# A graph convolution on one core: the two finishing stages of a chunk in their own memory bank, and the copy of a chunk's sum ahead of the next scalings

## The chip, the cores and the metric

The kernel runs on one core of a Trainium2 chip. The metric is the device time of one execution in microseconds (us); lower is better. The engines are TensorE (PE: matmuls; its weight loads are PEld), VectorE (DVE), ScalarE (ACT), GpSimd (POOL) and SyncE (SP). Each runs its own list of instructions in order, and instructions of different engines wait for each other through semaphores. Here SP issues ordinary DMA transfers and POOL issues the gathers (indirect DMAs, one for 128 rows). Matmuls write to PSUM, which ACT and DVE read.

## What is computed

A residual network on a graph of 6250 nodes with 128 features and 200000 edges sorted by their target node. Two layers follow each other: a graph attention layer, and an equivariant convolution. The change touches the second alone. Cut to what matters, with `x0`, `x1` linear maps of the normalized node features:

```python
e0 = f0[edge_src]; e1 = f1[edge_src]             # gather of source rows, 32 scalars and 32 vectors
h = gelu(gelu(edge_scalar_attr @ W_mlp1 * c) @ W_mlp2 * c2)
w = einsum('pxu,ex->epu', W_tp, h) * c2          # four weights per channel and edge
m0 = w[:, 0] * e0 * a0[:, None]                  # a0: first edge attribute, a1: the other three
m1 = w[:, 3] * einsum('eui,ei->eu', e1, a1) * INV_SQRT3
m2 = w[:, 1, :, None] * e0[:, :, None] * a1[:, None, :]
m3 = w[:, 2, :, None] * e1 * a0[:, None, None]
agg = zeros((N, 256)).at[edge_dst].add(concatenate([m0, m1, m2, m3], axis=1))
out = x + [COS * self + SIN * agg @ Wf]          # per irreducible part
```

## The kernel before, in words

The attention layer takes the first 2310 us or so and is the same in both kernels. Then a short stage builds a table of 128 values per node, and the edge loop of the convolution follows (L1632 to L1657), from about 2430 us to the end.

**Tiles.** A tile is 128 edges; there are NT = 1563. A group is SB = 8 tiles (196 groups), and one pass of the loop works on one group. A chunk is CT = 24 tiles, three groups; the 66 chunks cover 66 ranges of target nodes. I call the three groups of a chunk the first, second and third.

**One group.** `fetch` (L1611) gathers the source rows into a buffer `G` (L353, eight gathers on POOL; six buffers) and lets ACT scale them by `a0` (`scaled`, L1492, eight activations at L1495, result `g`). `layers` (L1588) loads the edge scalars `a8t` (L1595, two DMAs on SP, four buffers) and starts `hidden` (L1467), whose two layers are a matmul (L1476) into a PSUM bank with the tag "layer" (two buffers) and a Gelu on ACT (L1479, `hid`) each. `weigh` (L1483) turns the second layer's result into the weights, 8 pairs of matmuls (L1488) into a bank `big` (two buffers). `messages` (L1498) is DVE's part: seven instructions from L1508 to L1517; L1512 is the first that reads `big`, into a small tile `w`. The result `mess` has three buffers. `one_hot3` (L1523) compares target numbers with a row of slots. `scatter` (L1528) adds the messages with 8 pairs of matmuls (L1531) into the chunk's sum `whole` in PSUM, of which there is one.

**One chunk.** The first group of the next chunk closes a chunk: `close` (L1558) copies the sum to `acc` on ACT (L1561), and loads the chunk's own node features `xb` (L1564). The seventh tile of the next chunk adds the part of that sum that belongs to its nodes (`sink`, L1569; L1577 on DVE, L1579 on PE). `finish3` (L1533) is a generator in two stages. The first transposes the sum by matmuls (L1539) and copies it on ACT (L1541, `at`). The second multiplies by the last weights (L1544), adds `xb` by a matmul with the identity (L1545), copies on ACT (L1547, `o`, one buffer) and issues the output DMA (L1548). Both stages get their PSUM from outside: the bank `pw` that the weigh of the same pass then writes too, at other columns of the same tile.

**Order.** Most instructions are recorded through `keep`, which makes each engine run them in the order of the program. In one pass that order is: messages, the second layer of an earlier group, the first layer of group g+4, `fetch` of group g+1, a waiting stage of `finish3`, `close` where a chunk ends, `weigh` for group g+2, scatter. So ACT runs in the first group of a chunk: eight scalings, the copy of the sum, two activations; in the second: scalings, `at`, two activations; in the third: scalings, `o`, two activations. A stage's matmuls stand ahead of weigh on PE. SP runs its list in order too: two loads of `a8t` per group, and the loads of `xb`, the loads of attributes `a4` (L1603) and the output DMAs between them.

Of the kernel before, what the change touches and what calls it, by code (L numbers as in the profile page):

```python
# [31 lines left out]
F32 = mybir.dt.float32  # L32
# [11 lines left out]
P = 128  # L44
# [6 lines left out]
CT, LT = 24, 40  # L51
# [13 lines left out]
def gnn_kernel(ctx: ExitStack, tc: tile.TileContext, x, src, dst, attr4, attr8,  # L65
# [4 lines left out]
    N, D = x.shape  # L70
# [29 lines left out]
    NCH = -(-NT // CT)  # L100
# [14 lines left out]
    def big():  # L115
        return ps_big.tile([P, 8, P], F32, tag="big", name="big")
# [1080 lines left out]
    for now in range(NGR * MS + 1):  # L1197
        g, m = divmod(now, MS)
# [112 lines left out]
    with tc.tile_pool(name="att2", bufs=1) as pool, tc.tile_pool(name="dense", bufs=2) as dense, \  # L1311
# [68 lines left out]
        for b0 in range(0, NB, 2):  # L1380
            n = min(2, NB - b0)
# [13 lines left out]
            for h0 in range(0, NB, HS):  # L1395
# [7 lines left out]
                c = ct[:, :n, :, h0:h0 + HS, :].rearrange("p k a h d -> p h (k a) d")  # L1403
                parts = [t[:, :, :n * P].rearrange("p h (a d) -> p h a d", d=QN) for t in (ramp, up, down)]
# [14 lines left out]
            parts = dense.tile([P, 2, 2, R2], F32, name="parts")  # L1419
            acc = acc[:, :n, :2 * C2].rearrange("p k (j c) -> p k j c", j=2)  # L1420
            for k in range(n):
                b = b0 + k
# [28 lines left out]
    cw = ctx.enter_context(tc.tile_pool(name="cw", bufs=2))  # L1451
# [4 lines left out]
    ps_kept = ctx.enter_context(tc.tile_pool(name="ps_kept", bufs=1, space=PSUM))  # L1456
# [26 lines left out]
    def weigh(n, hid, pw):  # L1483

        for j in range(min(n, NPR)):
            for c in range(j, n, NPR):
                half = slice(c // NPR * HID, (c // NPR + 1) * HID)
                keep(nc.tensor.matmul(pw[:, c, :], hid[half, j * P:(j + 1) * P],  # L1488
                           wtp_sb[half].rearrange("x p u -> x (p u)"), start=True, stop=True))
        return pw  # L1490
# [39 lines left out]
            acc, start, stop = sink(c)  # L1530
            keep(nc.tensor.matmul(acc, oh[:, c, :], ms[:, c].rearrange("e h i u -> e (h i u)"), start=start, stop=stop))  # L1531

    def finish3(parts, xb, to):  # L1533


        ps = yield
        for j in range(2):
            for i, a in enumerate(parts):
                keep(nc.tensor.matmul(ps[:, j, :], a[:, j * D:(j + 1) * D], ident, start=i == 0, stop=i == len(parts) - 1))  # L1539
        at = cw.tile([P, 2, D], F32, name="at")  # L1540
        keep(nc.scalar.copy(at, ps[:, :2, :]))  # L1541
        ps = yield
        for j in range(2):
            keep(nc.tensor.matmul(ps[:, 0, :], at[:, j, :], wo_sb[:, j, :], start=j == 0, stop=False))  # L1544
        keep(nc.tensor.matmul(ps[:, 0, :], ident, xb, start=False, stop=True))  # L1545
        o = cw.tile([P, D], F32, name="o", bufs=1)
        keep(nc.scalar.copy(o, ps[:, 0, :]))  # L1547
        nc.sync.dma_start(to, o[:to.shape[0], :])  # L1548
        yield

    with tc.tile_pool(name="conv", bufs=1) as pool, tc.tile_pool(name="gath3", bufs=6) as gath:
        def first_node(c):
            return nc.values_load(base_i[0:1, c:c + 1], engines=[SP], min_val=0, max_val=N - P,
                                  skip_runtime_bounds_check_because="clamped to this range where it is computed")

        state, todo = {}, deque()

        def close(c):  # L1558

            a = cw.tile([P, 2 * D], F32, name="acc3")  # L1560
            keep(nc.scalar.copy(a, state["acc"]))  # L1561
            state["sums"] = [a]
            xb = cw.tile([P, D], F32, name="xb")
            nc.sync.dma_start(xb, xtd[ds(first_node(c), P), :])  # L1564
            ending = finish3(state["sums"], xb, out[ds(first_node(c), P), :])
            next(ending)
            todo.extend([ending, ending])

        def sink(t):  # L1569
            c, k = divmod(t, CT)  # L1570
# [11 lines left out]
        groups = [(t, min(SB, NT - t)) for t in range(0, NT, SB)]  # L1582

        def hots(g):
            t, n = groups[g]
            return one_hot3(dstc[:, t:t + n], n, cw.tile([P, SB, P], F32, name="ohr", bufs=4))

        def layers(g):  # L1588
            if g >= len(groups):
                return iter(())  # L1590
            t, n = groups[g]
            a8t = cw.tile([2 * NRAD, NPR * P], F32, name="a8t", bufs=4)
            for j in range(2 if n > NPR else 1):
                c = (t + j * NPR) * P
                nc.sync.dma_start(a8t[j * NRAD:(j + 1) * NRAD, :], attr8_t[:, c:c + NPR * P])  # L1595
            return hidden(n, a8t)
# [8 lines left out]
        def keep_a1(t):  # L1605
            m = min(LT, NT - t)
            a1s = kept[:, P + t // LT % 2 * 3 * LT:P + (t // LT % 2 + 1) * 3 * LT].rearrange("p (k f) -> p k f", f=3)
            keep(nc.vector.tensor_copy(a1s[:, :m], a4s[t][:, :m, 1:]))
            return a1s

        def fetch(g):  # L1611
            t, n = groups[g]
            if t % LT == 0 and t + LT < NT:
                load_a4(t + LT)
            G = gath.tile([P, SB, D], F32, tag="G", name="G")
            gather(G, table3, srcc[:, t:t + n], n)
            return G, scaled(G, n, a4s[t // LT * LT][:, t % LT:t % LT + n, 0:1])
# [3 lines left out]
        hids, pws = deque(), deque()  # L1621
# [10 lines left out]
        for g, (t, n) in enumerate(groups):  # L1632
            G, g0 = rows
            i = t % LT
            last = g + 1 == len(groups)
            ms, after = messages(G, g0, n, a1s[:, i:i + n, :], pws.popleft(), None if last else lambda: hots(g + 1),
                                 lambda: None)
            if i + SB == LT and t + SB < NT:
                a1s = keep_a1(t + SB)
            next(second, None)  # L1640
            first = layers(g + 4)
            next(first, None)
            if not last:
                rows = fetch(g + 1)
            weighing = hids.popleft() if hids else None
            pw = big() if weighing is not None or todo else None
            if todo:
                todo.popleft().send(pw)
            if t and t % CT == 0:
                close(t // CT - 1)  # L1650
            hids.extend(list(second)[-1:])
            next(first, None)
            if weighing is not None:
                pws.append(weigh(groups[g + 2][1], weighing, pw))
            scatter(ms, oh, range(n), lambda c: sink(t + c))
            second = first
            oh = after  # L1657
        close(NCH - 1)
        while todo:
            todo.popleft().send(big())  # L1660

        tot3 = pool.tile([P, 2 * D], F32, name="tot3")
        base = pool.tile([P, 1], F32, name="base")

        def general3(b, n):
            nc.vector.tensor_copy(base, starts[:, ds(b, 1)])
            nc.vector.memset(tot3, 0.0)
            with tc.For_i(0, NCHUNK, 1) as i:
                si, di = load_chunk(i)
                dl = work.tile([P, GK], F32, name="dl")  # L1670
                nc.vector.tensor_scalar(dl, di, base, None, op0=OP.subtract)
                at = []
                for f, attr in ((4, attr4), (NRAD, attr8)):
                    t = cw.tile([P, GK, f], F32, name=f"a{f}g")
                    nc.vector.memset(t, 0.0)
                    nc.sync.dma_start(t[:GP], attr[ds(i * (GP * GK), GP * GK), :].rearrange(
                        "(p k) f -> p k f", p=GP))
                    at.append(t)
                acc = whole()[:, :2 * D]
                for s in range(0, GK, GSB):  # L1680
                    cs = slice(s, s + GSB)
                    G = gath.tile([P, SB, D], F32, tag="G", name="Gg")
                    gather(G, table3, si[:, cs], GSB)
                    pa = big().rearrange("p c u -> p (c u)")
                    for c in range(GSB):
                        nc.tensor.transpose(pa[:NRAD, c * P:(c + 1) * P], at[1][:, s + c, :], ident)
                    a8t = cw.tile([2 * NRAD, NPR * P], F32, name="a8t", bufs=4)
                    nc.scalar.copy(a8t[:NRAD, :GSB * P], pa[:NRAD, :GSB * P])
                    pw = weigh(GSB, list(hidden(GSB, a8t))[-1], big())
                    ms, oh = messages(G, scaled(G, GSB, at[0][:, cs, 0:1]), GSB, at[0][:, cs, 1:], pw, lambda: one_hot(  # L1690
                        dl[:, cs], GSB, cw.tile([P, SB, P], F32, name="ohr", bufs=4)), lambda: None)
                    scatter(ms, oh, range(GSB), lambda c: (acc, s + c == 0, s + c == GK - 1))
                nc.vector.tensor_add(tot3, tot3, acc)
            xb = cw.tile([P, D], F32, name="xb")
            nc.vector.tensor_copy(xb, xt[:, ds(b, 1), :].rearrange("p o f -> p (o f)"))
            ending = finish3([tot3], xb, out[ds(b * P, n), :])
            next(ending)
            for _ in range(2):
                ending.send(big())

        with tc.If(flag_of(again3[0:1, 0:1]) > 0):
            with tc.For_i(0, FULL, 1) as b:
# [72 lines left out]
```

## Time and profile before

| what | value |
|---|---|
| median of 3 runs | 4809.09 us (4805.12 to 4830.14) |
| profiled execution, its own time | 4877.21 us |
| its span, first to last instruction | 4875.4 us |
| mean granted TensorE clock | 0.799 |
| attention and preparation | to about 2430 us |
| edge loop, full chunks | 2432.8 to 4802.5 us |
| its end | 4802.5 to 4875.4 us |
| PE, DVE, ACT, POOL busy, share of the span | 66%, 60%, 50%, 51% |
| gathers of the convolution (L353) | 1563, of 946 ns each |

The profile is one execution. It is about 1.4% longer than the median; durations are taken from it, and sums are made against its own time first. The profile's groups give for each line its instructions, busy time, the mean of one, and the idle time of the engine before them with what ended it. A releaser is inferred from semaphores; "remote" stands where the trace has no event for it, and "issue" where the engine waited for nothing that is seen. The timeline lists instructions with start and duration in us, and in brackets the idle time ahead and its releaser. Ends of matmuls are modelled.

### The profile page before, as it was taken

What the parts mean: (1) busy time and instruction counts of PE and PEld (TensorE: products, weight loads), DVE (VectorE), ACT (ScalarE), POOL (GpSimd) and SP (SyncE); (2) the same over time, 40 slices, a digit from 0 to 9 for tenths busy, and PEclk for the clock granted to TensorE, in tenths of its full rate; (3) what the DMA queues carried; (4) which work ended last, traced back from release to release, by engine and by line L of the source; (5) the groups of instructions that cost most, each with busy time, mean ns of one, the idle gap of its engine ahead of it and who ended that gap; (6) DMA issues with size and microseconds to landing.
All of it is one profiled execution on the core that took longest, in us unless ns stands there. A gap on an engine that the chain in (4) does not pass through costs nothing.

```text
span 4875.4 us, 63641 instructions
## 1 busy us (share of the span) xinstructions
PE 3212.9 (66%) x21302; PEld 2421.0 (50%) x21303; DVE 2937.8 (60%) x4901; ACT 2425.5 (50%) x5811; POOL 2501.5 (51%) x2440
## 2 busy tenths in 40 slices
PE   3247667777667789997466566665666666665667
PEld 3135545555445578886244444444444444444445
DVE  5457888888778779997244444444444444444445
ACT  3228788878778769997222222222322222222233
POOL 3556666657555600001655655555655555555553
PEclk7558888888788879998677777777787777877778
DMA  3346666767566554442111111111111111111111
GB/s 100 89 123 170 176 178 178 186 174 194 158 161 173 160 216 160 173 173 94 44 48 49 48 48 48 48 47 49 49 50 48 47 48 47 49 48 49 47 48 30
DMA packets 420347, 491.22 MB, mean 101 GB/s; under 512 B 267937, under 2 KB 303628, under 8 KB 419998
## 3 DMA queue, kind: packets, MB, share of 16 engines
q1 hardware_dynamic: 340900, 345.68, 23.8%
q0 software_dynamic: 78304, 139.36, 12.2%
q8 instruction: 175, 2.87, 0.2%
q10 hardware_dynamic: 794, 1.88, 0.1%
q14 instruction: 174, 1.43, 0.1%
HBM read 383.20 MB, written 103.42 MB: 100 GB/s over the span
## 4 chain that ended last, share of the span: by engine, by line
PE 23%; another core or an unknown queue 22%; ACT 4%; issue 3%; DVE 0%; DMA 0%; ACTq 0%; DVEq 0%
PE whole L1531 12%; PE layer L1476 5%; PE big L1488 4%; ACT g L1495 3%; ACT hid L1479 1%; PE big L1539 1%; PE whole L1579 1%; ACT o L1547 0%; PE big L1544 0%; ACT at L1541 0%; PE big L1545 0%; DVE mess L1517 0%; DMA out_x<-o 0%; ACT L1479 0%
## 5 line engine op out<-in xcount | busy, mean ns | idle before, releaser
L353 POOL DMA_INDIRECT G<-table,srcc x1563 | 1478.4, 946 | 1581.1 <-issue 626.5
L353 POOL DMA_INDIRECT G<-table,srcw x808 | 962.7, 1192 | 619.4 <-DVE msg L394 293.6
L1531 PE MATMUL whole<-mess,ohr 128*128 128x256 f32 x3126 | 838.6, 423 | 36.4 <-issue 24.6
L1488 PE MATMUL big<-wtp_sb,hid 64*128 64x128 f32 x3126 | 292.4, 335 | 856.3 <-ACT o L1547 739.6
L1512 DVE TENSOR_TENSOR w<-big,G 128x256 f32<-128x256 f32 x196 | 82.5, 421 | 1283.8 <-PE big L1488 764.9
L1096 ACT ACTIVATE up<-erb,sel 128x512 bf16<-128x512 f32 x1176 | 813.3, 744 | 1.0 <-PE small L878 1.0
L1531 PEld LDWEIGHTS whole<-mess,ohr 128*128 128x128 f32 x3126 | 648.6, 213 | 167.1 <-issue 41.7
L1488 PEld LDWEIGHTS big<-wtp_sb,hid 64*128 64x128 f32 x3126 | 245.3, 232 | 937.3 <-ACT o L1547 750.7
L878 PE MATMUL small<-key,lo 128*128 128x98 bf16 x3136 | 314.4, 231 | 379.2 <-issue 163.2
L860 ACT CAST ca<-small 128x392 bf16<-128x392 f32 x784 | 387.9, 498 | 297.6 <-remote 134.6
L1547 ACT COPY o<-big 128x128 f32<-128x128 f32 x66 | 17.6, 266 | 1038.4 <-remote 976.5
L878 PEld LDWEIGHTS <-lo 128*128 128x128 bf16 x3136 | 285.2, 123 | 469.9 <-issue 436.3
L1011 PE MATMUL up<-up,rc 128*102 128x512 bf16 x1176 | 474.5, 436 | 42.5 <-DVE up L1020 12.2
L1495 ACT ACTIVATE g<-G,a 128x128 f32<-128x128 f32 x1563 | 478.0, 401 | 0.0
L1401 ACT ACTIVATE ramp<-erb,sel 128x256 bf16<-128x256 f32 (+1 forms) x1138 | 461.1, 517 | 14.3 <-DVE up L1409 8.0
L1020 DVE TENSOR_TENSOR up<-up,ctc 128x3584 bf16<-128x3584 bf16 x168 | 339.5, 2021 | 59.6 <-issue 26.0
L1160 PEld LDWEIGHTS whole<-msg,ohr 128*128 128x128 f32 x1616 | 332.3, 244 | 62.8 <-issue 21.7
L852 DVE TENSOR_TENSOR lo<-slots,turned 128x2048 bf16<-128x2048 bf16 x196 | 238.8, 1218 | 162.9 <-PE small L878 72.3
L1160 PE MATMUL whole<-msg,ohr 128*128 128x68 f32 x1616 | 326.5, 317 | 1.3 <-ACT ring L1166 0.8
L1479 ACT ACTIVATE hid<-layer 128x512 f32<-128x512 f32 x392 | 220.7, 601 | 159.1 <-remote 63.8
L1014 PE MATMUL every<-ctc,rc 128*103 128x512 bf16 x588 | 256.4, 436 | 1.1 <-issue 1.0
L1414 PE MATMUL big<-rhs,up 128*128 128x196 bf16 x2401 | 239.8, 250 | 9.6 <-DVE up L1409 9.0
(316 smaller groups left out, 5112.8 us busy)
## 6 DMA issues: line engine op xcount, KB each, us to landing
counts<-ca SPq DMA_DIRECT2D x196, 392.0 KB
ct<-counts SPq DMA_DIRECT2D x196, 392.0 KB
ctc<-counts SPq DMA_DIRECT2D x1344, 56.0 KB
rc<-rhs SPq DMA_DIRECT2D x84, 358.8 KB
oht<-dlow SPq DMA_DIRECT2D x50, 512.0 KB
G<-table,srcc POOLq DMA_INDIRECT x1563
G<-table,srcw POOLq DMA_INDIRECT x808
a8t<-attr_rows SPq DMA_DIRECT2D x391, 16.0 KB
```

What stands on the lines that cost most here:

```text
L353: nc.gpsimd.indirect_dma_start(out=G[:, c, :], out_offset=None, in_=table, in_offset=bass.IndirectOffsetOnAxis(ap=idx[:, c:c + 1], axis=0))
L860: nc.scalar.copy(ca[:, :, k * W:(k + WBANK) * W].rearrange("p h (k d) -> p h k d", d=W), ps[:, :WBANK * NKEY].rearrange("p (k h d) -> p h ...
L878: nc.tensor.matmul(ps[:, n * NKEY:(n + 1) * NKEY], lo[:, a, :, r], ky[:, a, :, r], start=True, stop=True)
L1011: nc.tensor.matmul(sums["ups"][j][:2 * C1, :], r[:, i, c:c + 2 * C1], up[:, i], start=h0 + i == 0, stop=h0 + i == NB - 1)
L1020: nc.vector.tensor_tensor(by_part, by_part, state["ct", p, h0].rearrange("p k a h d -> p h (k a) d"), op=OP.min)
L1096: nc.scalar.activation(up[:, i], state["erb", p][:, j], AF.Relu, bias=sel1[:, h0 + i, 2 * q + j:2 * q + j + 1], scale=STEEP)
L1160: nc.tensor.matmul(kept1["acc"], ohs[g][:, t, :], mss[g][:, t], start=g * SB + t == first_of(c), stop=g * SB + t + 1 == last_of(c))
L1401: nc.scalar.activation(ramp[:, h, :n * P], erb[:, :n * P], AF.Relu, bias=sel2[:, h0 + h, :], scale=STEEP)
L1479: keep(nc.scalar.activation(x[:, :npr * P], ph, AF.Gelu_apprx_tanh, scale=1.0 / math.sqrt(size)))
L1488: keep(nc.tensor.matmul(pw[:, c, :], hid[half, j * P:(j + 1) * P], wtp_sb[half].rearrange("x p u -> x (p u)"), start=True, stop=True))
L1495: keep(nc.scalar.activation(g0[:, c], G[:, c, :], AF.Copy, scale=a0[:, c, :]))
L1531: keep(nc.tensor.matmul(acc, oh[:, c, :], ms[:, c].rearrange("e h i u -> e (h i u)"), start=start, stop=stop))
```

## The change

`finish3` takes its PSUM from the layers' two banks (`small_bank`), in place of the bank of weigh. Its stages are taken up at fixed passes: one, two and six passes after the pass that closes the chunk (`todo` is a dictionary by pass, `proceed`), and each stands after weigh and before the scatter of its pass. At the sixth only the output DMA is issued; `o` has two buffers. `close`, with the copy of the sum on ACT and the load of `xb`, now stands ahead of `fetch` of the next group, so ACT's order is, in the first group of a chunk: the copy of the sum, eight scalings, two activations; in the second: scalings, two activations, `at`; in the third: scalings, two activations, `o`. The counts of matmuls, activations and DMAs stay. The address of the output is formed when its DMA is issued (`place`). What the general path `general3` calls is adapted; it isn't run with these inputs.

```diff
-    def finish3(parts, xb, to):
-        ps = yield
+    def small_bank():
+        bank = ps_kept.tile([P, 4 * P], F32, tag="layer", name="layer", bufs=2)
+        return bank.rearrange("p (j f) -> p j f", f=P)
+
+    def finish3(parts, xb, place):
+        yield
+        ps = small_bank()
         for j in range(2):
             for i, a in enumerate(parts):
                 keep(nc.tensor.matmul(ps[:, j, :], a[:, j * D:(j + 1) * D], ident, start=i == 0, stop=i == len(parts) - 1))
         at = cw.tile([P, 2, D], F32, name="at")
         keep(nc.scalar.copy(at, ps[:, :2, :]))
-        ps = yield
+        yield
+        ps = small_bank()
...
-        o = cw.tile([P, D], F32, name="o", bufs=1)
+        o = cw.tile([P, D], F32, name="o", bufs=2)
         keep(nc.scalar.copy(o, ps[:, 0, :]))
+        yield
+        to = place()
         nc.sync.dma_start(to, o[:to.shape[0], :])
         yield
...
-        state, todo = {}, deque()
-        def close(c):
+        state, todo = {}, {}
+        def close(c, g):
             a = cw.tile([P, 2 * D], F32, name="acc3")
             keep(nc.scalar.copy(a, state["acc"]))
...
-            ending = finish3(state["sums"], xb, out[ds(first_node(c), P), :])
+            ending = finish3(state["sums"], xb, lambda: out[ds(first_node(c), P), :])
             next(ending)
-            todo.extend([ending, ending])
+            for ahead in (1, 2, 6):
+                todo.setdefault(g + ahead, []).append(ending)
+
+        def proceed(g):
+            for ending in todo.pop(g, []):
+                next(ending)
...
+            if t and t % CT == 0:
+                close(t // CT - 1, g)
             if not last:
                 rows = fetch(g + 1)
             weighing = hids.popleft() if hids else None
-            pw = big() if weighing is not None or todo else None
-            if todo:
-                todo.popleft().send(pw)
-            if t and t % CT == 0:
-                close(t // CT - 1)
             hids.extend(list(second)[-1:])
             next(first, None)
             if weighing is not None:
-                pws.append(weigh(groups[g + 2][1], weighing, pw))
+                pws.append(weigh(groups[g + 2][1], weighing, big()))
+            proceed(g)
             scatter(ms, oh, range(n), lambda c: sink(t + c))
...
-        close(NCH - 1)
-        while todo:
-            todo.popleft().send(big())
+        close(NCH - 1, len(groups))
+        for g in sorted(todo):
+            proceed(g)
```

More of the change, by code (lines that the diff above doesn't have):

```diff
@@ L1695, in general3 @@
             nc.vector.tensor_copy(xb, xt[:, ds(b, 1), :].rearrange("p o f -> p (o f)"))
[L1696 to L1699, printed above, removed]
+            for _ in finish3([tot3], xb, lambda: out[ds(b * P, n), :]):
+                pass
         with tc.If(flag_of(again3[0:1, 0:1]) > 0):
```

## The prediction

> **What bounds the kernel now.** I read the windows view first, for where the time lies, then the groups of instructions and the waits of the convolution's part, then its timeline. The steady part of the edge loop is 2432.8 to 4802.5 us (columns: sum, then busy time with its number of instructions for PE, PEld, DVE, ACT, POOL; granted clock; DMA share; GB/s):
>
> ```profile
> 2432.80:4802.50 2369.70, 1499.21 (x7320) 1060.98 (x7320) 1099.27 (x1562) 680.56 (x2013) 1384.43 (x1464) 0.79 0.19 48
> ```
>
> 1464 gathers are 61 chunks of 24, so a chunk takes 2369.70 / 61 = **38.85 us**. Per chunk PE is busy 24.6, DVE 18.0, ACT 11.2 and POOL 22.7: no engine is full, and the bound is a chain of waits. POOL is nearest. Its group of the same part (columns: count, busy time and mean ns of one, then idle time and who ended it):
>
> ```profile
> L353 POOL DMA_INDIRECT G<-table,srcc x1529 | 1446.2, 946 | 1030.0 <-issue 616.4 <-ACT g L1495 395.7 <-ACT hid L1479 10.3
> ```
>
> A gather takes 0.946 us and the next follows 0.30 later: 24 x 1.25 = 30.0 us a chunk. The other 8.85 are two pauses, because all six G buffers are full: counted in the trace, 58 runs of 16 gathers end in a pause of 6.6 on average (to 7.0), 63 runs of 8 in one of 2.9. Two chunks at the common beat: 48 x 1.25 - 4 x 0.30 = 58.8 of runs, 2 x 7.0 + 2 x 2.9 of pauses, together 78.6, so 39.3 each. The waits say who keeps the buffers (total us, times, longest):
>
> ```profile
> ACT o L1547 <- remote: 976.5, 54, 23.5
> DVE w L1512 <- PE big L1488: 764.9, 58, 15.1
> ...
> PE big L1488 <- ACT o L1547: 739.6, 58, 17.3
> ...
> POOL G L353 <- ACT g L1495: 395.7, 59, 13.9
> ...
> ACT acc L1561 <- PE whole L1531: 151.4, 43, 4.6
> ...
> PE big L1488 <- ACT at L1541: 52.4, 59, 14.1
> ```
>
> Read upward, that is one chain, once a chunk: POOL waits for scalings (L1495) that stand on ACT behind `o` (L1547); PE's weigh (L1488) waits for `o`, because both share the bank `pw`; DVE waits for weigh. "Remote" hides what `o` waits for. The timeline (start, duration, instruction, idle before it) shows it:
>
> ```profile
> 3639.11 0.39 PE L1545 MATMUL big<-xb,ident 128*128 128x128 f32 x2
> ...
> 3649.76 0.61 SPq L1595 DMA_DIRECT2D a8t<-attr_rows  x2
> 3650.00 0.95 POOL L353 DMA_INDIRECT G<-table,srcc  x1 [0.30 <-issue]
> 3654.09 0.27 ACT L1547 COPY o<-big 128x128 f32<-128x128 f32 x1 [18.91 <-remote]
> ...
> 3654.41 2.08 PE L1488 MATMUL big<-wtp_sb,hid 64*128 64x128 f32 x16 [14.91 <-ACT o L1547]
> 3655.22 2.45 ACT L1495 ACTIVATE g<-G,a 128x128 f32<-128x128 f32 x8
> ...
> 3656.53 0.42 DVE L1512 TENSOR_TENSOR w<-big,G 128x256 f32<-128x256 f32 x1 [13.97 <-PE big L1488]
> ...
> 3657.93 0.95 POOL L353 DMA_INDIRECT G<-table,srcc  x1 [6.98 <-ACT g L1495]
> ```
>
> PE's last matmul for `o` ends at 3639.50 and ACT starts 14.6 us later, 3.1 after the run of gathers ended at 3650.95. The old output DMA is no cause ("out_x<-o" ends 1.2 us of ACT's waits in all). So PE's signal arrives late. I matched each wait to its releaser: PE's signals are late at 53 of 65 `o` copies (median 13.8 us), DVE's and ACT's never by more than 0.04. They are late where SP issued a DMA inside a running run of gathers (103 of 103 from 8 us after it), until 1.7 us (run of 8) or 3.1 us (run of 16) past the run's end; without an issue in the run, 20 of 233. This is a correlation, not a proved cause.
>
> A rule that speaks against this reading is in the Trainium skill, "SBUF — State Buffer", section "Who interferes with whom": DMA never contends with a compute engine, PE and ACT wait on nobody. The late starts above measure something that this rule doesn't explain; if it covered signals too, freeing the bank would free all, and rival 3 would be the sum.
>
> **The change, part by part.** Counts of instructions stay as they are on PE, DVE and ACT; only waits and order move.
>
> (a) *Stages in a bank of the layers.* Weigh no longer shares a bank with `at` and `o`: the 739.6 + 52.4 us of PE's waits go. They lie on POOL's chain only once a chunk, so the gain isn't their sum. What is next: PE runs on through weigh and scatter while signals are late, so at 3654 the weigh (2.08 us) is already done; DVE is released with ACT and no longer 2.4 us after it. POOL's pause then ends with the scalings: `o` 0.27, the sum's copy 0.37, eight scalings 2.45, instead of `o`, two activations (1.09) and scalings. 3654.09 + 3.09 + 0.26 = 3657.4 against 3657.93: a pause of about 6.5, or less where the run's tail overlaps it, down to 4.8 by the rows (the 2.1 us of weigh gone whole). The larger part is the pattern: with PE ahead, a first layer's matmul (L1476), whose end lets SP issue the next a8t, moves out of the run into POOL's pause at every other chunk; that run has no late signals, DVE frees two buffers during it, and the next run is of 16 in place of 8. My cycle by hand over two chunks: three runs of 16, 48 x 1.25 - 3 x 0.30 = 59.1, pauses 5.1 to 6.5, 4.8 to 6.2 and 2.9: 71.9 to 74.7, so 36.0 to 37.4 a chunk, middle 36.65. Gain 2.2 x 61 = **-134 us** (-88 to -174).
>
> New waits: three users now rotate through two layer banks. The first layer of each chunk's third group waits for `at`, that of the next chunk's first group for `o`; L1539 and L1544 wait for an activation (0.60) of their own iteration. No row shows this wait; below, L1476 now waits 50.6 us in two long cases and else nothing (0); above, it inherits the whole 739.6. I take 0 beyond the cycle, since the layers run two groups ahead of weigh; 739.6 / 58 = 12.8 a chunk is the far end, and it is no more than today's wait moved to another line, so no loss below today's 38.85 follows from it alone.
>
> (b) *The sum's copy ahead of the scalings.* ACT in the first group of a chunk: copy, eight scalings, two activations; before, scalings, copy, activations. All that is queued behind the copy (2.45 of scalings, 1.2 of activations) now waits for the last scatter (L1531). Before, the copy waited 151.4 (43) on it and with "issue" and "remote" 288.8 us in 64: 4.5 each. Covered: +0.37 or nothing, as in the cycle. Uncovered: +4.5 + 0.37 = 4.9 a chunk, +300 us. I take covered, since DVE runs two groups ahead of PE (three `mess` buffers) and PE has run on: at 3654 its scatter is done. Gain bound: scatter of the next chunk waits 11.8 + 12.6 us in all for this copy; at most -24.
>
> (c) *`o` with two buffers, output DMA four groups later.* The wait it removes is 1.2 us in all: 0. On SP the output DMA moves past four or more a8t loads and stands behind the x rows' load; its waits for `o` (125.0 us in 43 times) go, since `o` is then long done, and a8t loads, two issues a group, come that much earlier. Those were for four groups ahead, so nobody waits for them (one case, 9.3 us). Worth 0, bounds -9 and, if issues land in other runs, the rivals below.
>
> (d) *Tail.* The last output DMA was issued at 4870.7 and ended the span at 4875.4, 4.7 us. Now up to three are issued there one behind another: 0 to +3. I take +1.
>
> A second page bears on (a): by "TensorE: Matmul & The Clock Gate", Part 1, an idle window halves PE's clock. The rows agree (weigh 2.08 after a wait, 1.16 without; scatter 4.67 to 5.5 against 3.72). By that rule less idle PE would be worth (0.92 + 1.8) x 61 = 165 us, an estimate; mine sets it at nothing beyond the pause, since POOL sets the pace.
>
> Sum: 0 (counts) - 134 + 0 + 0 + 1 = -133 on the profiled execution of 4877 (span 4875.4): 4744. That execution lies 1.4% over the median of 4809.09; the same gain against the median gives 4676, rounded **4680**.
>
> **The rivals.**
> 1. *The late signals only move.* PE runs on, but `o` still starts at the run's end and the scalings stand behind it on ACT; runs of 16 and 8 stay. For: (a)'s own 3657.4 against 3657.93. Per chunk 0 to -0.5: -30 to 0, time 4780 to 4815.
> 2. *Slower: the sum's copy blocks the scalings.* Place: ACT, first group of a chunk, where `o`, copy and scalings now stand in this order, the first two both waiting for PE. If the copy needs a scatter whose signal comes 4 us after POOL would have restarted, G buffers are freed one by one: runs of 8 alone, 24 x 1.25 - 3 x 0.3 = 29.1 and pauses 2.9 + 5.5 + 6.2, or 43.7: +4.85 x 61 = +296, time 5105. It decides from the point at which the copy starts over 2.2 us (the cycle's gain) later than the scalings used to. Once every third chunk it is +75 or so: 4885. For: 4.5 us of wait at this copy today. Against: PE runs ahead.
> 3. *The late state goes altogether,* since no PE wait holds the first layers back and SP issues only in pauses. Then POOL alone: 30.0 a chunk, -8.85 x 61 = -540, time 4270. Against: a8t loads stay two a group, and runs are longer than pauses.
> 4. *The change does not do what it says:* the built order of instructions has the stages' matmuls behind weigh, in the layer banks, and the copy ahead of the scalings, so I give it nothing.
>
> **How the numbers follow.** The cycle (a gain of 60 to 230, the -88 to -174 of (a) widened by its two edges, the scatter's -24 and a milder pattern; 4580 to 4750) 0.50; rival 1 0.20; rival 2 0.22 (a third of it the full 43.7); rival 3 0.08, and its milder half is 4500. A measurement here tells 0.5% (24 us) from no change. Faster: 0.50 + 0.06 of rival 1 + 0.08 = 0.64; same: 0.13 of rival 1 and 0.02 of rival 2; the rest slower, 0.21. The range goes from 4500 to 4900: it leaves out the full rival 2 (0.08) and most of rival 3 (0.06); the cycle's own range is 4580 to 4750.
>
> **What would show it.** Right: "PE big <- ACT o" gone from the waits; more runs of 16 than of 8 by two to one or more; POOL's wait for ACT g under 250 us; 36 to 37.4 us a chunk. Rival 1: `o`'s wait of about 970 us stays, weigh's goes, pauses unchanged. Rival 2: the wait of L1561 far above 290 us and POOL's wait for the scalings above 395.7. Rival 3: `o`'s wait below 100. My weakest step is the pattern in (a): it rests on a correlation with SP's issues; if late signals have another cause, only the 0.5 us of the pause remains.

## The result and the profile after

The changed kernel takes 4981.51 us (median of 4, 4967.94 to 5001.39) against 4817.66 for the kernel before (4 runs), a ratio of **1.0314**, interval 1.0278 to 1.0351. The forecast was 4680, faster; the time lies 81 us above the range.

The steady part of the edge loop first, in the windows view, for 58 chunks (1392 gathers; columns as in the prediction):

```profile
2461.00:4854.80 2393.80, 1490.69 (x6951) 1043.83 (x6949) 1045.76 (x1485) 647.39 (x1915) 1316.64 (x1392) 0.76 0.17 45
```

2393.80 / 58 = 41.3 us a chunk, in place of 38.85. From the first gather to the last it is 2656 us against 2518, so 137 more; the profiled span grew by only 99.6, since what stands ahead, the same in both kernels, took 35.5 us less in this execution. POOL's group of the convolution:

```profile
L353 POOL DMA_INDIRECT G<-table,srcc x1512 | 1430.2, 946 | 1148.9 <-ACT g L1495 697.9 <-issue 419.1 <-ACT hid L1479 18.2
```

A gather still takes 946 ns, but POOL's waits for the scalings went up from 395.7 to 697.9. Counted in the trace, the runs of gathers changed too: 27 of 24 with a pause of 14.3 us behind them, 38 of 16 with 5.4, 30 of 8 with 4.1. The common cycle of two chunks is one of each: 48 x 1.25 - 3 x 0.30 = 59.1 of runs, and pauses of 14.5 + 5.5 + 4.1 = 24.1, so 83.2, or 41.6 a chunk. The waits of the changed kernel's convolution, counted from 2300 us on (the row above is from 2340 us on; us, times, longest):

```profile
DVE mess L1514 <- ACT g L1495: 821.2, 118, 51.2
POOL G L353 <- ACT g L1495: 711.6, 92, 15.5
ACT at L1546 <- remote: 683.3, 54, 16.2
...
ACT hid L1479 <- remote: 576.2, 34, 52.8
...
PE layer L1476 <- ACT at L1546: 329.1, 36, 11.3
...
PE layer L1550 <- ACT hid L1479: 277.8, 28, 16.6
...
PE big L1488 <- issue: 171.9, 91, 3.1
...
PE layer L1476 <- issue: 115.9, 42, 9.2
```

PE's weigh no longer waits for `o`: that line, 739.6 us before, is gone. In its place PE waits 329.1 us at a first layer for `at`, and 277.8 at the second stage for `hid`, both because three users share two layer banks. The last two rows are idle time of PE itself, before matmuls that wait for nothing the trace shows; the kernel before had 63.8 and 6.2 us of it. The timeline shows what that does to one long pause:

```profile
4153.27 1.02 PE L1476 MATMUL layer<-hid,wm_sb 128*128 128x512 f32 x2
...
4173.48 0.94 POOL L353 DMA_INDIRECT G<-table,srcc  x1 [0.30 <-issue]
4178.86 1.09 ACT L1479 ACTIVATE hid<-layer 128x512 f32<-128x512 f32 x2 [15.67 <-remote]
...
4179.51 1.23 PE L1550 MATMUL layer<-wo_sb,at 128*128 128x128 f32 x4 [7.39 <-ACT hid L1479]
...
4180.95 5.42 PE L1531 MATMUL whole<-mess,ohr 128*128 128x256 f32 x16
...
4186.41 0.37 ACT L1569 COPY acc<-whole 128x256 f32<-128x256 f32 x1 [4.95 <-PE whole L1531]
4186.68 2.44 ACT L1495 ACTIVATE g<-G,a 128x128 f32<-128x128 f32 x8
...
4189.39 0.94 POOL L353 DMA_INDIRECT G<-table,srcc  x1 [14.96 <-ACT g L1495]
```

The layer's matmul ends at 4154.29; ACT's `hid` starts 24.6 us later, 4.43 behind the end of the run of gathers. Then everything stands in a row: `hid` frees the bank (0.65), the second stage (1.44), the scatter (5.42 at a granted clock of 0.66, against 3.62 at 1.00 from 4149.82 on), the sum's copy (0.31 to its end as the scalings see it), eight scalings (2.44), POOL (0.27): 14.96 us.

### The profile page after: what moved, and what is told of

Its sections match the earlier page's. It is cut to its first block, busy times and chain, and to the rows that moved or that the text cites. A ratio compares the mean times of both kernels' runs of the same rounds, so it can differ in the third digit from the quotient of the medians.

```text
span 4974.9 us, 63463 instructions
## 1 busy us (share of the span) xinstructions
PE 3280.2 (66%) x21302; PEld 2458.0 (49%) x21303; DVE 2936.6 (59%) x4901; ACT 2424.4 (49%) x5811; POOL 2506.7 (50%) x2440
## 4 chain that ended last, share of the span: by engine, by line
another core or an unknown queue 26%; PE 21%; ACT 5%; issue 2%; DMA 0%; ACTq 0%
PE whole L1531 10%; PE layer L1476 6%; ACT g L1495 3%; PE big L1488 3%; ACT hid L1479 2%; PE layer L1550 1%; PE layer L1551 1%; PE whole L1592 0%; ACT at L1546 0%; PE layer L1544 0%; ACT acc L1569 0%; DMA G<-table,srcc 0%; ACT o L1553 0%; ACTq L1479 0%
## 5 line engine op out<-in xcount | busy, mean ns | idle before, releaser
L1531 PE MATMUL whole<-mess,ohr 128*128 128x256 f32 x3126 | 805.5, 410 | 55.1 <-issue 44.3
L1531 PEld LDWEIGHTS whole<-mess,ohr 128*128 128x128 f32 x3126 | 637.7, 210 | 157.6 <-issue 50.7
L1514 DVE TENSOR_TENSOR mess<-big,g 128x768 f32<-128x768 f32 x196 | 186.5, 951 | 847.1 <-ACT g L1495 821.2
L1479 ACT ACTIVATE hid<-layer 128x512 f32<-128x512 f32 x392 | 217.2, 587 | 726.3 <-remote 576.2
L1476 PE MATMUL layer<-a8t,wm_sb 16*128 16x512 f32 x392 | 275.4, 788 | 441.9 <-ACT at L1546 329.1
L1512 DVE TENSOR_TENSOR w<-big,G 128x256 f32<-128x256 f32 x196 | 81.7, 417 | 656.5 <-remote 633.7
L1488 PEld LDWEIGHTS big<-wtp_sb,hid 64*128 64x128 f32 x3126 | 260.3, 231 | 337.1 <-issue 333.3
L1488 PE MATMUL big<-wtp_sb,hid 64*128 64x128 f32 x3126 | 312.8, 333 | 172.3 <-issue 171.9
L1546 ACT COPY at<-layer 128x256 f32<-128x256 f32 x66 | 24.6, 372 | 733.2 <-remote 683.3
L1476 PEld LDWEIGHTS layer<-a8t,wm_sb 16*128 16x128 f32 x392 | 68.9, 217 | 602.5 <-ACT at L1546 360.8
```

The source lines that it names most:

```text
L1476: keep(nc.tensor.matmul(ph, w, x[:, :npr * P], start=True, stop=True))
```

## The experiments

The runs fell on several chips, and these differ. On chips 2, 3, 7 and 8 the kernel before takes 3981 to 3983 us, on chip 13 4704, on chip 15 4807, on the first one (which the results don't number) 4818. The changed kernel as it stands ran on the first chip and on chips 3 and 7. Ratios are always against the kernel before on the same chip.

| edit | chips 2, 3, 7, 8 | chip 13 | chip 15 |
|---|---|---|---|
| kernel before, us | 3981 to 3983 | 4704.5 | 4806.7 |
| changed kernel | 0.9992 [0.9982, 1.0001], twice | not run | not run |
| changed, copy back behind the scalings | 0.9993 and 1.0001 | 1.0115 [1.0085, 1.0145] | |
| before, copy alone moved ahead | 1.0006 [0.9994, 1.0017] | 1.0268 [1.0229, 1.0306] | |
| changed, second stage in the slots' bank | 1.0005 [0.9992, 1.0017] | 1.0902 [1.0879, 1.0925] | |
| changed, a8t for 12 groups at once | 1.0013 [1.0003, 1.0024] | 4769 to 4881 us, too far apart for a ratio | |
| before, with iotas of 128 / 1024 columns between gathers | 1.0132 [1.0115, 1.0148] / 1.0867 [1.0849, 1.0885] | | |
| hold by hand: before / changed / copy back / slots' bank, us | | | 5062 / 5493 / 5266 / 5875 |

**Single parts, on chip 8.** My theory B: a long pause is made by two things in a row, PE's scatter held by a stage that waits for its layer bank, and the copy, ahead of the scalings, waiting for that scatter. The rivals were each of these alone. Theory A is the prediction's: SP's issues start the late signals.

> The changed kernel with the edge scalars a8t loaded for 12 groups by two DMAs, where it had two DMAs for every group; SP issues 0.5 of them a chunk in place of 6, none tied to a matmul inside a run of gathers. Theory A (a DMA that SP issues inside a run of gathers starts the state of late PE signals): the late state is nearly gone, the waits of at, o and hid on remote fall from 1300 us to under 300, POOL's pauses shrink and the chunk goes from 41.6 to 30 to 34 us: 4290 to 4520 us. Rival (the gathers alone make PE's signals late, SP's issues only coincide with them): the time stays within 1% of the changed kernel, 4930 to 5030, and the waits on remote stay above 1000 us.

> The changed kernel with only the copy of the sum (and xb's load) put back behind the scalings. Theory B (a pause of 15 us is made by two things in a row: PE's scatter is held by a stage that waits for its layer bank, and the copy, ahead of the scalings, waits for that scatter): the pause of 15 after a run of 24 falls to about 9.7, which is -2.65 a chunk: about 4820. Rival (only the wait for the layer banks costs): no change, 4950 to 5000. Rival (only the copy's place costs): the gain that was predicted appears, 4680 to 4780.

> The kernel before with only the copy of the sum put ahead of the scalings. Theory B: after the late signals come, o, weigh (2.1) and scatter (5.4) must end before the copy and so before the scalings, where scalings stood 1.1 us behind o: POOL restarts some 7 us later in each chunk, 5000 to 5250. Rival (the copy is covered, only the layer banks cost): 4800 to 4840.

> The changed kernel with the second stage (L1550, L1551) in free columns of the bank that holds the slots, so that it waits for no layer's activation and holds no layer bank; the first stage stays in a layer bank. Theory B: scatter of the third group no longer stands behind a wait for hid, so it has run when the late signals come, and the pause of 15 falls to about 8.6: -3.2 a chunk, about 4790. Rival (the copy's place alone costs): 4950 to 5000.

The edits, in this order and cut to what matters (KB is 12; with `False`, `close` leaves out the copy):

```diff
-            a8t = cw.tile([2 * NRAD, NPR * P], F32, name="a8t", bufs=4)
...
+            if g % KB == 0:
...
+                        a8s[b] = cw.tile([2 * NRAD, KB, NPR * P], F32, name="a8s", bufs=2)
...
+                            nc.sync.dma_start(a8s[b][j * NRAD:(j + 1) * NRAD, :m], cols[:, :, j, :])
+            return hidden(n, a8s[g // KB * KB][:, g % KB, :])
```

```diff
+            if not last:
+                rows = fetch(g + 1)
             if t and t % CT == 0:
                 close(t // CT - 1, g)
-            if not last:
-                rows = fetch(g + 1)
             weighing = hids.popleft() if hids else None
```

```diff
+            if t and t % CT == 0:
+                a = cw.tile([P, 2 * D], F32, name="acc3")
+                keep(nc.scalar.copy(a, state["acc"]))
+                state["sums"] = [a]
             if not last:
                 rows = fetch(g + 1)
...
-                close(t // CT - 1)
+                close(t // CT - 1, False)
```

```diff
-        ps = small_bank()
+        ps = kept[:, 3 * P:][:, None, :]
```

All four took 3979 to 3986 us, and so did the kernel before. No theory told of that. So the changed kernel itself was run next, on chip 3:

> The changed kernel itself, unedited, on the chip of these runs. Four variants of it ran here within 0.1% of the kernel before, all near 3980 us, where the first runs gave 4818 for the kernel before and 4982 for the changed one. Theory C (the late PE signals, and with them the whole cost of the change, belong to the first chip and not to the program): here POOL's gathers run without a pause and the changed kernel takes 3975 to 3990, ratio 1.000 within 0.2%. Rival (the change costs 2.65 us a chunk wherever it runs): 4140 us, ratio 1.04. If a chip with late signals is drawn: ratio 1.03 again, 4960 to 5000.

It took 3979.29 us against 3982.53, ratio 0.9992: theory C. POOL's group of the loop, from later runs of both on chip 7, first the kernel before, then the changed one:

```profile
L353 POOL DMA_INDIRECT G<-table,srcc x1174 | 1110.4, 946 | 358.0 <-issue 313.5 <-DVE dot L1510 35.7 <-DMA G<-table,srcc 4.9
```

```profile
L353 POOL DMA_INDIRECT G<-table,srcc x1177 | 1110.6, 944 | 358.7 <-issue 309.9 <-DVE dot L1510 36.0 <-ACT g L1495 6.7
```

A gather takes the same 0.95 us and 0.30 to the next, but there is one run of gathers from the first to the last: POOL's 30.0 us a chunk are the time, as in the prediction's third rival, for both kernels. The changed kernel's new waits are there as well, in its list of waits on that chip:

```profile
PE layer L1544 <- ACT hid L1479: 234.3, 48, 5.6
ACT acc L1569 <- PE whole L1531: 171.9, 49, 5.2
```

4.9 and 3.5 us a chunk, and POOL's pace is the same: here these waits reach nobody who sets the time. In this kernel a wait costs only where it reaches POOL.

**The late signals by hand.** To bring them to a chip without, gathers were written down six groups ahead and ACT held in each third group until the buffers were full:

```diff
+                if g % 3 == 2 and g + 6 < len(groups) - 1:
+                    held = cw.tile([P, 1], F32, name="held")
+                    keep(nc.scalar.copy(held, rowsG[g + 6][:, SB - 1, 0:1]))
+                    for _ in range(HOLD):
+                        keep(nc.scalar.copy(spent[:, 1], spent[:, 0]))
```

> The kernel before, with the late signals of the first chip made by hand: gathers are written down six groups ahead (the G buffers set the same limit), and in each chunk's third group, right behind the scalings, ACT waits for the last gather that is written down and then runs 22 copies without use, about 11 us, so that o, and all behind it on ACT, comes some 3 us after POOL has filled all six buffers. Baseline of the four. Behind the hold stand o 0.27, two activations 1.1, scalings 2.45: a pause of 6 to 7 us a chunk, 36 to 37.5 us in place of 30, and once 35 us to fill the buffers: 4390 to 4490 us. If the late signals are not what made POOL pause, the time stays near 3980.

> The changed kernel with the same hold by hand at the same place. Theory B: behind the hold stand two activations 1.1 (PE's stage waits for them, since its layer bank is held by hid), the stage 1.6, scatter 3.7 to 5.4, the sum's copy 0.37, scalings 2.45: a pause of 12 to 14, 42 to 44 us a chunk: 4750 to 4880, 300 or more above h_before. Rival (PE has run on, the copy is covered, as predicted): at or below h_before. Rival (the cost on the first chip is something else than these waits): within 60 us of h_before.

> As h_after, with only the sum's copy (and xb's load) put back behind the scalings. Theory B: behind the hold stand activations 1.1, the stage 1.6, o 0.27, scalings 2.45: a pause of 8 to 9, 38 to 39.5 a chunk: 4480 to 4600. Rival (the wait for the layer banks alone costs): as h_after. Rival (the copy's place alone costs): as h_before or below.

> As h_after, with only the second stage's matmuls moved out of the layer banks, into free columns of the bank that holds the slots. Theory B: PE's scatter of the third group runs during the hold, behind which stand activations 1.1, o 0.27, the copy 0.37, scalings 2.45: a pause of 6.5 to 7.5, 36.5 to 38 a chunk: 4420 to 4510. Rival (the copy's place alone costs): as h_after.

These fell on chip 15, where signals are late anyway, so the times (two runs each) hold both delays, all lie above their ranges, and only their order can be read: 5062, 5493, 5266, 5875. The first three stand in the order that theory B gives, the changed kernel 431 us above the kernel before, and the copy put back takes off 226 of these. h_o_kept went against it by far. Its waits say why:

```profile
DVE dot L1508 <- ACT o L1553: 2312.5, 64, 37.7
POOL G L353 <- ACT hid L1479: 1584.3, 63, 25.9
```

DVE reads its attributes from the same tile into which the stage now writes, so DVE waits for `o`, once a chunk. The edit put a worse wait where it took one away: it says nothing on the layer banks.

**The single parts where signals are late**, on chip 13:

> The changed kernel with only the copy of the sum (and xb's load) put back behind the scalings, once more, for a chip on which PE's signals come late (the kernel before near 4810). Theory B (layer-bank wait and copy in a row): the pause of 15 falls to about 9.7: about 4820, as before. Rival (only the wait for the layer banks costs): 4950 to 5000. Rival (only the copy's place costs): 4680 to 4780. On a chip without late signals: 3980 again.

> The kernel before with only the copy of the sum put ahead of the scalings, for a chip with late signals. Theory B: o, weigh and scatter must end before the copy and so before the scalings: 5000 to 5250. Rival (only the layer banks cost): 4800 to 4840. On a chip without late signals: 3980.

> The changed kernel with the second stage's matmuls in free columns of the slots' bank, for a chip with late signals. Theory B by its first form: about 4790, since scatter of the third group no longer waits for hid. But with the hold by hand this edit was the slowest of four (5875 against 5493), since PE, with nothing to wait for ahead of scatter, seems to fill the run with more work whose signals come late: by that the time is above the changed kernel's, 5000 to 5300. On a chip without late signals: 3980.

> The changed kernel with a8t loaded for 12 groups at once (SP issues 0.5 of these loads a chunk in place of 6), for a chip with late signals. Theory A (a DMA that SP issues inside a run of gathers starts the late state): 4290 to 4520. Rival (SP's issues only coincide with it): 4930 to 5030. On a chip without late signals: 3985.

The ranges were made for a kernel before near 4810 us; it took 4704 here, so only ratios can be held against them. The copy alone, moved ahead in the kernel before, costs 2.68%: more than nothing, so it isn't covered, and less than theory B's 4% and more. Three of its waits, on ACT's copy, on DVE and on POOL:

```profile
POOL G L353 <- ACT g L1495: 405.3, 45, 15.6
DVE mess L1514 <- ACT g L1495: 303.1, 62, 50.5
ACT acc L1645 <- PE whole L1531: 264.1, 43, 7.0
```

On the first chip the kernel before had 79.8 in DVE's line. The long pause comes with the copy: its trace has 13 runs of 24 gathers with 14.0 us behind them on average. On the first chip the changed kernel has 27 such runs, and the kernel before a single one, with 5.7 us behind it. With the copy put back, the changed kernel is 1.15% slower than the kernel before: what the layer banks and the stages' new places cost without the copy. Theory B had no change here, the copy's rival a gain of 1 to 3%, the layer banks' rival a loss of 3 to 4%: none was met. Its POOL group:

```profile
L353 POOL DMA_INDIRECT G<-table,srcc x1479 | 1395.3, 943 | 928.1 <-issue 491.8 <-ACT g L1495 225.3 <-ACT acc L1569 180.5
```

90 of its 96 runs are of 16 gathers and 2 of 24, with pauses of 6.1, 6.0 and 4.3 in turn: 59.1 + 16.4 = 75.5 for two chunks, 37.75 each (in the fastest of its four executions, 4721 us). That is the pattern of the prediction's cycle, a little above its 36.0 to 37.4. s_o_kept shows the false wait again (DVE for `o`, 1603.1 us in 63).

s_batch speaks against theory A, though its time lies in neither range. Its trace has 207 of SP's DMAs in the edge loop, where the changed kernel has 562, and its waits are these:

```profile
DVE w L1512 <- remote: 732.4, 78, 32.6
ACT hid L1479 <- remote: 613.1, 48, 37.7
...
ACT at L1546 <- remote: 426.2, 38, 14.6
```

The waits on "remote" stay far above theory A's 300 us, and PE's signals are late 131 times without any issue of SP in the run. So an issue of SP isn't needed for them. I then counted the waits on PE that fell into a run of gathers by how far into the run PE had finished; late is over 0.6 us:

```
us into the run   before (first chip)   after (first chip)   s_batch (13)   s_copy_back (13)
0 to 4            11 of 156             2 of 117             18 of 84       8 of 164
4 to 8            102 of 275            123 of 221           73 of 178      139 of 174
8 to 12           91 of 135             70 of 74             89 of 114      204 of 222
over 12           8 of 8                57 of 57             51 of 51       60 of 60
```

So the state goes with the time into a run of gathers, on these chips. Breaking the runs would try that:

> The kernel before with a small POOL instruction (an iota of 128 columns, about 0.9 us) after every four gathers of the convolution, kept in order, so that no run of gathers is longer than 5 us. On a chip with late signals, theory D (the late state builds up 4 to 8 us into a run of gathers back to back and ends with it, whatever SP does): the waits on remote and PE's late signals nearly go, POOL's pace of 24 x 1.25 + 6 x 1.2 = 37.2 us a chunk is the bound: 4680 to 4760 us, and POOL's waits for the scalings fall under 100 us. Rival (the late state goes with the mean rate of gathers, not with runs): late signals stay, POOL's pauses stay beside the new ones, 4900 or more. On a chip without late signals: POOL's pace alone, about 4430.

> As p_before, with an iota of 1024 columns in place of 128 after every four gathers: the short one took 0.26 us, which by width makes 1 to 2 us for this one, six of them 6 to 12 us a chunk, and POOL's own pace 36 to 42 us. On a chip with late signals, theory D (the late state builds up within a run of gathers back to back and ends with it): waits on remote under 300 us in all, DVE and ACT no longer late, the time set by POOL's pace alone, 4400 to 4750. Rival (it goes with the gathers whether they run back to back or not): waits on remote over 800 us and POOL's pauses beside the new ones, 4900 to 5200. On a chip without late signals: POOL's pace, 4350 to 4720, and nothing on this question.

```diff
+            spent = cw.tile([P, P], F32, name="spent", bufs=2)
+            return nc.gpsimd.iota(spent, pattern=[[1, P]], base=0, channel_multiplier=0,
...
-            gather(G, table3, srcc[:, t:t + n], n)
+            for c in range(0, n, 4):
...
+                keep(pause())
```

Both fell on chips without late signals and answer only the other half. The second has 1024 columns and one buffer. The iotas took 0.26 (where 0.9 was expected) and 1.00 us, the times were 1.3% and 8.7% over the kernel before. In the second the gap after every fourth gather is 1.17 us and not 0.30: 1563 / 4 x 0.87 = 340 us, measured 344. There, POOL's pace is the time. The last comparison, of three kernels on one chip, fell on chip 7 too:

> The kernel before, unedited, for its profile on the same chip as the next two. With late signals: 4700 to 4820, runs of 16 and 8 in alternation, or their mixture where it is nearer to 4700. Without: 3980.

> The changed kernel, unedited, on the same chip. With late signals: 2.5 to 3.5% over the kernel before; without: the same time.

> The changed kernel with only the sum's copy put back behind the scalings, on the same chip. With late signals, theory E (the copy's place makes most of the loss, the layer banks the smaller part): runs of 16 alone with pauses of 6.1, 6.0, 4.3, 37.8 us a chunk, so about 4750 whatever the kernel before takes there. Rival (the edit's time follows the chip): 1 to 1.5% over the kernel before on any chip. Without late signals: 3980.

3988.14 (one execution), 3977.77 and 3980.92: the same time, so theory E was not tried either. Thus the changed kernel's own 3.1% was measured on the first chip alone, the parts on chip 13, and their sum across chips (2.7 + 1.15 = 3.8, or 3.1 - 1.15 = 2.0 for the copy in the changed kernel) is an estimate.

## Why the prediction was wrong, by its own steps

**What bounds the kernel.** Right for the chip of its profile: waits, with POOL next, and late PE signals at the root. Wrong in tying the start to SP's issues: s_batch, and the chips on which SP issues inside one long run and nothing is late. "This is a correlation" was the right word, and the step that used it failed. Of the four signs named for being right only the first came, "PE big <- ACT o" gone: runs of 16 to runs of 8 stand 38 to 30 and not two to one, POOL's wait for `g` is 697.9 us and not under 250, a chunk 41.3 us. `o`'s wait on "remote" fell from 976.5 to 41.5 us, but late signals now hold `at`, `hid` and `w` (683.3, 576.2 and 633.7 us): the wait moved to other readers.

**(a) Bank of the layers.** "The 739.6 + 52.4 us of PE's waits go" held. "I take 0 beyond the cycle, since the layers run two groups ahead of weigh" failed: 329.1 + 277.8 = 607 us of PE's waits came back, 9.3 for each of 65 chunks, where the far end that was set aside is 12.8. The layers do run ahead, but late signals hold `at` and `hid`, and a bank is held as long as its reader waits. "No loss below today's 38.85 follows from it alone" isn't borne out either: with the copy put back the kernel is 1.15% slower than before. The cycle itself can be found. It came up in stretches of the changed kernel (runs of 16 from 3204 to 3306 us, pauses 6.3, 4.2, 6.4, 6.2) and throughout s_copy_back, 37.75 us where 36.0 to 37.4 was said; the third pause is 4.3, not 2.9. But it did not beat the kernel before on chip 13, of which there is no trace.

**(b) The copy ahead of the scalings.** This is the step that turned the sign: "I take covered, since ... PE has run on: at 3654 its scatter is done." It was not: in the pause shown the scatter starts at 4180.95, 6.5 us after the run of gathers ended, because the same change put the second stage, with its wait for `hid`, ahead of it. Nor does PE simply run on: before that, the last three matmuls of weigh start 2.8 us apart (4166.09, 4168.90, 4171.74) with nothing the trace shows to wait for. Two edits priced one by one as free are not free together: one holds the scatter, the other makes POOL wait for it. Even alone, without a stage in a layer bank, the copy costs 2.68% (chip 13), 115 us or 1.8 for each of 65 chunks, between the prices of 0 and 4.9 that stood there.

**(c), (d).** Not tried by themselves; the output DMA's waits for `o` fell from 125.0 us to 5.8.

**The clock.** The prediction set it at nothing beyond the pause, since POOL sets the pace. In the long pause PE is on POOL's path: 5.42 us for the scatter at a granted clock of 0.66, against 3.62 at 1.00, so 1.8 us, once in two chunks. That the clock falls after idle time is the rule of the Trainium skill, "TensorE: Matmul & The Clock Gate", Part 1; the rows agree (PE had been idle 7.39 us, and the clock was 0.50 from 4174.40 to 4180.95), and no run took the clock alone.

**The rivals.** The second had the right place and mechanism, ACT in the first group with the copy in front, and the right point, a copy later than the scalings used to be. It had 0.22. Its sign at the copy came only in part: L1569 waits 363 us in all, against 288.8 before, of which 150.8 for the scatter, no more than before. Its size was off in shape: not runs of 8 alone at 43.7, but one long pause in two chunks, 41.6. The milder form, "once every third chunk", was also summed wrongly: a third of 296 is 99 us and not 75, so 4908 and not 4885, and by that the range left out nearly all of this rival. The third rival, 30.0 us a chunk, is what chips 2, 3, 7 and 8 do, with and without the change; there the kernel before takes 3982, since the part ahead of the edge loop is shorter too, and a range made from one chip's profile couldn't hold it.

**Still open.** What makes PE's signals late on some chips: the runs tell when (mostly from 4 to 8 us into a run of gathers on) and what isn't needed (SP's issues), no more. Whether it is the chip itself or what else ran beside it is not shown, nor why PE's own matmuls come slowly late in a run. Shorter runs were not measured on such a chip. The changed kernel as it stands was not run on chip 13. The wait for the layer banks was not taken away cleanly; its 1.15% also holds the stages' new places on PE and ACT.

## What to carry to other kernels

When a wait for a shared buffer is taken away, list who holds the new buffer and for how long at the worst moment of the trace, not on average; and price two edits of one change together where one's cover is the other's victim. An in-order engine that feeds the pacing one should do that work first: a copy that waits for the longest chain doesn't belong ahead of it. And before a few per cent are explained, see whether the pacing engine has idle time at all on the chip at hand.

## What was not expected of the hardware

The same program took 3981 to 4818 us on different chips. Most of it lies in the convolution, but not all: its gathers run from 2297.5 to 4816.0 us in the first chip's profile of the kernel before and from 2010.2 to 3964.8 on chip 7, so 2518 against 1955 us; what stands ahead of them, the attention layer with gathers of its own, took 287 us more, and the end behind them 38. A gather takes 0.94 to 0.95 us on all of them. Where signals of PE come late, they were up to 24.6 us behind the matmul's end in the changed kernel's full chunks. PE went on with other instructions meanwhile, but late in a run it slowed down too (171.9 + 115.9 us of idle time that the trace explains by nothing, where chip 7 has no such row). I had forecast a change on such a chip without knowing that others are free of it.
